# Pacing the gathers of sparse entries by the matmuls of two passes, and a finer ring of row buffers

## The chip, the cores and the metric

The kernel runs on one core of a Trainium2 chip. The time is the device time of one execution in microseconds (us), the median of several executions. A core has these engines: TensorE for matmuls (PE in the profile; PEld is its loading of weights), VectorE (DVE), ScalarE (ACT), GpSimd (POOL) and SyncE (SP), which in this kernel only issues transfers. Sixteen DMA engines move the data. Each engine works through its own instructions in order, and waits on semaphores for what others do.

## The reference, cut to what matters

The reference is a graph network of two layers on 3327 nodes with 512 features. The adjacency matrix `adj` (fp32, values in 0.05 to 1, about a quarter of a per cent of it nonzero, denser towards the first nodes) is given as a dense matrix; the kernel reads its transpose `adjT`.

```python
# layer 0
h = relu(layernorm(x))
u = h @ W1                                  # 512 -> 128
g = relu(adj @ u + b1)
x = x + (adj @ g) @ W2 + b2
# layer 1
h = relu(layernorm(x))
attn_a = sigmoid(concat([adj @ h, h], 1) @ Wa.T + ba)
attn_b = sigmoid(concat([adj @ h, h], 1) @ Wb.T + bb)
hw = h @ W_sa
scores = (hw @ a_sa[0, :512])[:, None] + (hw @ a_sa[0, 512:])[None, :]
e = where(adj != 0, exp(-leaky_relu(scores, 0.01)), 0)
x_a = (e / (e.sum(1, keepdims=True) + 1e-5)) @ hw
x_b = adj @ (h @ W_gcnb) + b_gcnb
return x + sigmoid(attn_a * x_a + attn_b * x_b)
```

Layer 0 needs two products with `adj`, and the second needs all of the first. Layer 1 needs, for each node, the rows `h` of its neighbours, weighted once by `adj` and once by an exponential of scores that is zero where `adj` is zero.

## The kernel before

The nodes are padded to 3328 = 26 blocks of 128. The columns of `adjT` are taken in seven chunks, six of 512 and a last one of 256.

**Pass 1 (lines 442 to 486)** computes `adj @ u`. For each chunk c it goes through the 26 blocks j: `load_adj` (L197, on the SP queue) brings a tile of 128 x 512 entries (256 KB) into one of eight buffers, TensorE adds `u[j]` times the tile to `acc_u` (L466), and VectorE reduces the same tile to `most` (L467): the largest magnitude in each group of 32 columns, so that it is known which rows have anything nonzero in which group. In chunk 0 the blocks of `x` are loaded, normalized and multiplied as well. After a chunk's last matmul, `make_g` (L252) makes gT from the sum on ScalarE (L256) and turns it with `pg` (L259).

**The lists.** `make_lists` (L335) is a generator that makes, out of `most` of one chunk, the lists of nonzero rows, while the tiles of the next chunk go by (one `next` per tile from j = 2 on; for chunk 6, during pass 2's chunk 0). The 128 nodes of a block i ≥ 1 are four groups of 32: the half of the partitions says which half of the block, and `q` (0 or 1) which of the two groups in that half. A block has a fixed number of *rounds*, `rooms[i]`: 10, 8, 7, 6, 6, then five blocks of 5, twelve of 4 and three of 3, together 119. One round of one q is 128 row numbers, one per partition: 64 rows for each of two groups. So there are 238 columns of numbers: `row_h` (which row of h) and `row_a` (which 32 entries of `adjT`, L428). As soon as a batch of lists is made, `make_lists` issues on GpSimd all of its gathers of entries (L432 to L439, recorded at L327): an indirect transfer each, of 128 pieces of 32 numbers (128 bytes), into `ae[i]`, which is kept for every block until layer 1. That makes 238 *gathers of entries*, queued by batches.

**Pass 2 (L553 to L576)** is the same walk over `adjT` with `g` in place of `u` (L558). When a chunk's sum is complete, `make_h1` turns it (px, L524), adds `x`, normalizes, and writes the rows of h (512 numbers and a score) to `h_dram` (L531).

**The hub.** Block 0 is the densest and is combined in full, with `adjT`'s first columns and all rows of h (`combine_hub`, L141, L577 to L590).

**Layer 1 (L634 to L756).** For block i ≥ 1, `combine(i)` goes through segments of at most four rounds. A segment takes one buffer `hr` of eight rows of 520 numbers per partition, of which there are three; GpSimd gathers two rows per partition and round (128 x 2080 bytes each, L327): 238 *row gathers*. Then VectorE adds the scores (L652, one operation per q), `masked_exp` (L130) makes the exponentials from them and from the entries in `ae[i]`, and four matmuls per round (L671), each on half of the partitions, add both weighted sums. `turn(i)` (L678) transposes the sums, `weigh(i)` (L712) multiplies by `W_sa` (`p_a`, L717) and `W_g` (`p_b`, L722), and `finish` (L601) makes the output. The three are pipelined: combine of block i, turn of block i−1, weigh of block i−2. `weigh` takes four banks of PSUM of the pool psB: p_s for the column sums of e, p_a, and two of p_b, whose second uses 257 of 512 columns at most.

The buffers of pools are recycled: an instruction that writes to a buffer waits for the last readers of what stood in it. Within an engine, the order is the order of the program text, except where a priority or `issue_after` says otherwise.

Of the kernel before, what the change touches and what calls it, by code (L numbers as in the profile page):

```python
# [43 lines left out]
def kernel(  # L44
# [71 lines left out]
    hubp = ctx.enter_context(tc.tile_pool(name="hubp", bufs=LAG + 2))  # L116

    def ln_relu(dst, src, pool, name):
        stats = pool.tile([P, 6], F32, tag="bn6", name=f"bn_{name}", bufs=3)
# [65 lines left out]
    with (  # L185
# [137 lines left out]
            for t in ae[1:]:  # L323
                nc.gpsimd.memset(t[:, :, :GW], 0.0)

        def gather(dst, table, rows, last):
            nc.gpsimd.indirect_dma_start(  # L327
                out=dst, out_offset=None, in_=table,
                in_offset=bass.IndirectOffsetOnAxis(ap=rows, axis=0),
                bounds_check=last, oob_is_err=False,  # L330
            )

        adj_groups = adjT.rearrange("j (b i) -> (j b) i", i=GW)

        def make_lists(c, most):  # L335


# [48 lines left out]
            for batch in batches:  # L386
                col = {}
                m = 0
                for i, q in batch:
                    col[i, q] = m  # L390
                    m += rooms[i]
                f0 = first[batch[0][0]] + batch[0][1] * rooms[batch[0][0]]
                pl = bank(psB, f"p_list_{f0}")
                plv = pl[:, : m * NT].rearrange("p (c j) -> p c j", j=NT)
                for i, q in batch:
                    r = rooms[i]
                    at = l0w.tile(
                        [P, max(rooms), 2, HALF], BF16, tag="at", name=f"at_{i}_{q}", bufs=3
                    )
# [25 lines left out]
                nc.vector.tensor_scalar(  # L425
                    row_h[:, f0 : f0 + m], jb[:, :m], float(NP - 1), None, op0=ALU.min
                )
                nc.vector.scalar_tensor_tensor(  # L428
                    row_a[:, f0 : f0 + m], jb[:, :m], float(NG), group_col[:, f0 : f0 + m],
                    op0=ALU.mult, op1=ALU.add,  # L430
                )
                for i, q in batch:  # L432
                    for k0, k1 in segments(i):
                        for k in range(k0, k1):
                            f = f0 + col[i, q] + k
                            gather(
                                ae[i][:, 2 * k0 + q * (k1 - k0) + k - k0, :GW], adj_groups,
                                row_a[:, f : f + 1], NP * NG - 1,
                            )  # L439
                yield  # L440

        for i in range(4):
# [8 lines left out]
        for c in range(NCH):  # L451
# [3 lines left out]
            for j in range(NB):  # L455
                if c == 0:
                    if j + 4 < NB:
                        load_x(j + 4)
                    if j + 3 < NB:
                        normalize(j + 3)  # L460
                    if j + 2 < NB:
                        turn_h(j + 2)
                    if j + 1 < NB:
                        make_u(j + 1)
                a = load_adj(j, c, "a1")
                nc.tensor.matmul(acc[:, :w], u[j], a[:, :w], start=(j == 0), stop=(j == NB - 1))  # L466
# [86 lines left out]
        for c in range(NCH):  # L553
            c0, w = chunks[c]
            acc = bank(psA, f"acc_g_{c}")
            for j in range(NB):
                a = load_adj(j, c, "a2")
                nc.tensor.matmul(  # L558
                    acc[:, :w], g[j], a[:, :w], start=(j == 0), stop=(j == NB - 1)
                )  # L560
# [66 lines left out]
    with tc.tile_pool(name="spw", bufs=2) as spw:  # L627
# [6 lines left out]
        def combine(i):  # L634
# [3 lines left out]
            r = rooms[i]  # L638
            acc = [bank(psA, f"acc_{i}_{h}") for h in range(2)]
            es = spw.tile([P, 2, GW], F32, tag="es", name=f"es_{i}")  # L640
            for k0, k1 in segments(i):
# [6 lines left out]
                both = ae[i][:, 2 * k0 : 2 * k1, :]  # L648
                e = both[:, :, GW:]
                s_l = s_left[i * P // CW][:, i % (CW // P), :].rearrange("p (q i) -> p q i", q=2)  # L650
# [16 lines left out]
                for k in range(n):  # L667
                    for q in range(2):
                        for h in range(2):
                            half_p = slice(h * HALF, (h + 1) * HALF)  # L670
                            nc.tensor.matmul(  # L671
                                acc[h][q * HALF : (q + 1) * HALF, :], both[half_p, q * n + k, :],
                                hr[half_p, q * n + k, :D],
                                start=(k0 + k == 0), stop=(k1 == r and k == n - 1),
                            )
            return acc, es

        def turn(i, ty, tyT):  # L678
# [16 lines left out]
                        tyT[:, :, h, :], pt.rearrange("p (k n) -> p k n", k=KD)  # L695
                    )

        def add_up(i, es):

            p_s = bank(psB, f"p_s_{i}")  # L700
            if i:
                for h in range(2):
                    half_p = slice(h * HALF, (h + 1) * HALF)
                    nc.tensor.matmul(
                        p_s[half_p, 0:1], es[half_p].rearrange("p q i -> p (q i)"), ones[half_p],
                        start=True, stop=True,
                    )
            else:
                nc.tensor.matmul(p_s[:, 0:1], es, ones, start=True, stop=True)
            return p_s  # L710

        def weigh(i, tyT, es):  # L712
            p_s = add_up(i, es)
            p_a = bank(psB, f"p_a_{i}")
            p_b = [bank(psB, f"p_b_{i}_{k}") for k in range(2)]
            for k in range(KD):
# [3 lines left out]
            for n in range(2):  # L720
                for k in range(KD):
# [1 line left out]
                        p_b[n][:, :WH], tyT[:, k, 0, :], W_g_sb[:, k, n * WH : (n + 1) * WH],  # L723
                        start=(k == 0), stop=(k == KD - 1),
                    )
            finish(spw, i, p_a, p_b, p_s[:, 0:1])

        turning, weighing = None, None
        for i in [*range(NB), None, None]:
# [15 lines left out]
                weigh(*weighing)  # L745
            weighing = (b, tyT, es) if turning is not None else None
            turning = made

    over = nc.values_load(overflow[0:1, 0:1], min_val=0, max_val=1)
    with tc.If(over > 0):  # L750
# [124 lines left out]
```

## Time and profile before

| | |
|---|---|
| median of 3 executions | 1151.23 us (1142.97 to 1166.88) |
| span of the profiled execution | 1129.3 us |
| busy: PE, DVE, POOL, PEld, ACT | 856.7, 530.2, 527.3, 422.6, 189.9 us |
| mean granted clock of TensorE | 0.868 |
| moved by DMA | 216.54 MB, 192 GB/s on average |

The stages, by the first and last instructions of their lines: chunk 0 of pass 1 to 88 us, chunks 1 to 6 to 447, a transition to pass 2's steady walk to 484, pass 2 to 667, the hub to 734, layer 1 to the end.

How to read the page: its slices are fortieths of the span (28.2 us), each digit the busy tenths of an engine, or the granted clock of TensorE in tenths (PEclk), or the share of time that the DMA engines are busy. In the groups, after the count come the busy time, the mean time of one instruction in ns, then the idle time of the engine right before these instructions and what ended most of it. "issue" means that the engine waited for nothing that the profile shows. "remote", or another core or an unknown queue, means that the releaser could not be named. A matmul in fp32 is recorded as two instructions, so 182 matmuls of a pass are 364.

### The profile page before, as it was taken

Reading aid. Unit: us, or ns where it says so; the run is one execution under the profiler, and the core shown is the slowest. Engines: PE = TensorE matmul, PEld = TensorE weight load, DVE = VectorE, ACT = ScalarE, POOL = GpSimd, SP = SyncE. Lnnn points to the kernel's source line nnn. Section 1 sums busy time; section 2 is a strip of 40 time slices with the busy share of each in tenths; the row PEclk is TensorE's granted clock in tenths of the full one; section 3 lists DMA queues with packets and bytes.
Section 4 is the critical chain, followed back from the end, with each engine's and each line's share of the span. In section 5 each row is a group of like instructions: output and inputs, shape, how many; then the busy total and the mean of one; then the engine's idle time right before and its main releaser. Section 6 shows DMA issues by size and latency. Waiting matters only on the chain.

```text
span 1129.3 us, 12108 instructions
## 1 busy us (share of the span) xinstructions
PE 856.7 (76%) x3639; PEld 422.6 (37%) x3639; DVE 530.2 (47%) x1593; ACT 189.9 (17%) x405; POOL 527.3 (47%) x559
## 2 busy tenths in 40 slices
PE   4898428256382917399999977858998989999996
PEld 3663103012030304144343443323554445555554
DVE  5656215234262715236566676412454444454543
ACT  4560000000000000002111131100222122223232
POOL 6543764736647464540000005166766676666400
PEclk9999657658586958599999999888999989999998
DMA  6797227144263514289999968676777777877511
GB/s 220 265 278 242 50 63 230 29 136 118 57 205 100 170 46 137 81 268 367 320 347 347 334 233 273 171 213 175 202 221 215 217 208 213 215 211 217 177 57 41
DMA packets 116105, 216.54 MB, mean 192 GB/s; under 512 B 18849, under 2 KB 32448, under 8 KB 116032
## 3 DMA queue, kind: packets, MB, share of 16 engines
q1 hardware_dynamic: 82368, 138.27, 37.8%
q0 software_dynamic: 26656, 66.41, 21.8%
q10 hardware_dynamic: 7008, 11.02, 2.8%
q8 instruction: 31, 0.51, 0.2%
q14 instruction: 42, 0.34, 0.1%
HBM read 189.14 MB, written 27.37 MB: 192 GB/s over the span
## 4 chain that ended last, share of the span: by engine, by line
another core or an unknown queue 22%; PE 22%; issue 16%; DMA 15%; POOL 14%; DVE 7%; ACT 2%; SPq 1%; POOLq 0%; ACTq 0%; DVEq 0%
POOL hr L327 12%; PE acc_g L558 9%; DMA a<-in_adjT_dram 8%; DMA hr<-h_rows,row_h 4%; PE acc_u L466 4%; PE p_a L717 2%; PE p_b L722 2%; PE acc L671 1%; DVE most L467 1%; PE px L524 1%; DMA xb<-x 1%; POOL x L230 1%; DMA x<-in_x_dram 1%; ACT hrow L128 1%
## 5 line engine op out<-in xcount | busy, mean ns | idle before, releaser
L327 POOL DMA_INDIRECT hr<-h_rows,row_h x238 | 243.6, 1024 | 324.3 <-DMA a_hub<-in_adjT_dram 184.6
L327 POOL DMA_INDIRECT ae<-in_adjT_dram,row_a x238 | 238.7, 1003 | 182.3 <-issue 70.1
L466 PE MATMUL acc_u<-a,u 128*128 128x512 f32 (+1 forms) x364 | 208.4, 694 | 91.7 <-DMA a<-in_adjT_dram 80.9
L467 DVE TENSOR_REDUCE most<-a 128x16 f32<-128x512 f32 (+1 forms) x182 | 112.6, 641 | 125.5 <-DMA a<-in_adjT_dram 123.8
L558 PE MATMUL acc_g<-a,g 128*128 128x512 f32 (+1 forms) x364 | 159.5, 590 | 9.5 <-DMA a<-in_adjT_dram 9.4
L671 PE MATMUL acc<-hr,ae 64*64 64x512 f32 x952 | 136.8, 624 | 26.5 <-issue 10.5
L466 PEld LDWEIGHTS acc_u<-a,u 128*128 128x128 f32 x364 | 71.3, 223 | 168.6 <-DMA a<-in_adjT_dram 115.4
L558 PEld LDWEIGHTS acc_g<-a,g 128*128 128x128 f32 x364 | 69.8, 198 | 88.4 <-issue 62.3
L717 PE MATMUL p_a<-W_sa_sb,tyT 128*128 128x512 f32 x208 | 97.1, 610 | 1.6 <-DVE f L608 1.2
L722 PE MATMUL p_b<-W_g_sb,tyT 128*128 128x257 f32 x416 | 94.7, 379 | 0.3 <-issue 0.3
L722 PEld LDWEIGHTS p_b<-W_g_sb,tyT 128*128 128x128 f32 x416 | 78.6, 189 | 23.2 <-issue 12.4
L652 DVE TENSOR_TENSOR ae<-s_left,hr 128x128 f32<-128x128 f32 (+2 forms) x72 | 19.4, 269 | 142.0 <-DMA hr<-h_rows,row_h 132.2
L671 PEld LDWEIGHTS acc<-hr,ae 64*64 64x64 f32 x952 | 44.6, 137 | 104.6 <-issue 82.7
L512 DVE SCALAR_TENSOR_TENSOR junk<-hrow,w_rows 128x512 f32<-128x512 f32 x104 | 71.5, 688 | 4.5 <-ACT hrow L128 1.9
L256 ACT ACTIVATE gT<-acc_u,b_col 128x512 f32<-128x512 f32 (+1 forms) x7 | 4.6, 657 | 374.8 <-remote 258.4
L259 PE MATMUL pg<-ident,gT 128*128 128x128 f32 x26 | 6.9, 410 | 78.8 <-ACT gT L256 61.8
L717 PEld LDWEIGHTS p_a<-W_sa_sb,tyT 128*128 128x128 f32 x208 | 37.7, 191 | 39.9 <-issue 38.2
L526 DVE TENSOR_TENSOR x<-px,xb 128x512 f32<-128x512 f32 x26 | 17.8, 684 | 67.8 <-PE px L524 58.9
L230 POOL TENSOR_TENSOR x<-x,b_row 128x512 f32<-128x512 f32 x26 | 32.9, 1276 | 34.9 <-ACT h L128 20.9
L415 DVE TENSOR_TENSOR past<-p_list,place_col 128x416 f32<-128x416 f32 (+7 forms) x17 | 9.1, 537 | 73.0 <-remote 51.2
L133 ACT ACTIVATE ae<-ae 128x256 f32<-128x256 f32 (+2 forms) x36 | 13.7, 379 | 155.4 <-DVE ae L132 79.1
L247 PE MATMUL pu<-W_sb,hT 128*128 128x128 f32 x208 | 31.1, 297 | 7.9 <-ACT hT L241 7.9
(126 smaller groups left out, 849.8 us busy)
## 6 DMA issues: line engine op xcount, KB each, us to landing
a<-in_adjT_dram SPq DMA_DIRECT2D x312, 256.0 KB
h_rows<-hrow SPq DMA_DIRECT2D x26, 260.0 KB
h_hub<-h_rows SPq DMA_DIRECT2D x26, 260.0 KB
x<-in_x_dram SPq DMA_DIRECT2D x26, 256.0 KB
xb<-x SPq DMA_DIRECT2D x26, 256.0 KB
xb<-xb SPq DMA_DIRECT2D x26, 256.0 KB
a<-in_adjT_dram SPq DMA_DIRECT2D x52, 128.0 KB
x<-x ACTq DMA_DIRECT2D x26, 256.0 KB
```

Source lines behind the costliest of these rows:

```text
L230: nc.gpsimd.tensor_tensor(xs[i], xs[i], b2_row, ALU.add)
L247: nc.tensor.matmul(pu[:, :HID], hT[:, k, :], W1_sb[:, k, :], start=(k == 0), stop=(k == KD - 1))
L327: nc.gpsimd.indirect_dma_start(out=dst, out_offset=None, in_=table, in_offset=bass.IndirectOffsetOnAxis(ap=rows, axis=0), bounds_check=las ...
L466: nc.tensor.matmul(acc[:, :w], u[j], a[:, :w], start=(j == 0), stop=(j == NB - 1))
L467: nc.vector.tensor_reduce(most[:, : w // GW, j], a[:, :w].rearrange("p (b i) -> p b i", i=GW), axis=AX.X, op=ALU.max, apply_absolute_value ...
L512: return nc.vector.scalar_tensor_tensor(junk, h, 1.0, w_rows[:, s, :], op0=ALU.mult, op1=ALU.mult, accum_out=into)
L526: nc.vector.tensor_tensor(x1, px, xi, ALU.add)
L558: nc.tensor.matmul(acc[:, :w], g[j], a[:, :w], start=(j == 0), stop=(j == NB - 1))
L652: nc.vector.tensor_tensor(e[:, q * n : (q + 1) * n, :], s_l[:, q, :].unsqueeze(1).to_broadcast([P, n, GW]), hr[:, q * n : (q + 1) * n, D : ...
L671: nc.tensor.matmul(acc[h][q * HALF : (q + 1) * HALF, :], both[half_p, q * n + k, :], hr[half_p, q * n + k, :D], start=(k0 + k == 0), stop= ...
L717: nc.tensor.matmul(p_a, tyT[:, k, 1, :], W_sa_sb[:, k, :], start=(k == 0), stop=(k == KD - 1))
L722: nc.tensor.matmul(p_b[n][:, :WH], tyT[:, k, 0, :], W_g_sb[:, k, n * WH : (n + 1) * WH], start=(k == 0), stop=(k == KD - 1),)
```

## The change

It has three parts.

1. **Gathers of entries are paced.** `make_lists` no longer issues them; it only notes which lists are ready (`listed`). A generator, `gather_adj`, yields them one at a time in the order in which layer 1 will need them. `gather_behind(matmul)` takes the next one and makes it wait for that matmul. Pass 1 calls it for every odd tile (one per two tiles; if the list in question isn't ready, the slot passes unused), pass 2 for three of each four tiles. What is left is issued in layer 1, two per block, behind the block's last row gather. What it is for: the gathers come one at a time among the tiles, rather than by batches in a row.
2. **Row buffers by rounds.** `hr` is now a buffer of two rows (one round), and there are 16 of them, 32 rows in place of 24. A buffer comes free when its round's four matmuls are done, rather than with the whole segment. The score addition is one operation per round, over both q.
3. **The column sum** p_s goes into the last column of the second p_b's bank, behind p_b's matmuls, so `weigh` takes three banks.

```diff
-        def gather(dst, table, rows, last):
...
+    listed = set()
+    def gather_adj():
+        for i in range(1, NB):
+            r = rooms[i]
+            for k0, k1 in segments(i):
+                for q in range(2):
+                    for k in range(k0, k1):
+                        while (i, q) not in listed:
+                            yield None
+                        f = first[i] + q * r + k
+                        yield gather(
+                            ae[i][:, 2 * k0 + q * (k1 - k0) + k - k0, :GW], adj_groups,
+                            row_a[:, f : f + 1], NP * NG - 1,
+                        )
+    columns = gather_adj()
+    def gather_behind(matmul):
+        g = next(columns, None)
+        if g is not None:
+            tc.add_manual_dep(
+                g.ins, matmul.ins.name,
+                mybir.DependencyInfo(mybir.DependencyClass.Sync, mybir.DependencyReason.DATA),
+                reason="pace",
+            )
...
-                for i, q in batch:
-                    for k0, k1 in segments(i):
-                        for k in range(k0, k1):
-                            f = f0 + col[i, q] + k
-                            gather(
-                                ae[i][:, 2 * k0 + q * (k1 - k0) + k - k0, :GW], adj_groups,
-                                row_a[:, f : f + 1], NP * NG - 1,
-                            )
+                listed.update(batch)
                 yield
...
                 if j >= 2:
                     next(lists, None)
+                if j % 2:
+                    gather_behind(added)
...
                 if c == 0 and j >= 2:
                     next(lists, None)
+                if (c * NB + j) % 4 != 3:
+                    gather_behind(added)
...
-                hr = spw.tile([P, 2 * SEG, ROW], F32, tag="hr", name=f"hr_{i}_{k0}", bufs=3)
+                hr = []
                 for k in range(n):
+                    hr.append(spw.tile([P, 2, ROW], F32, tag="hr", name=f"hr_{i}_{k0 + k}", bufs=16))
                     for q in range(2):
                         f = first[i] + q * r + k0 + k
-                        gather(hr[:, q * n + k, :], h_dram[:, :], row_h[:, f : f + 1], NP - 1)
...
-                for q in range(2):
+                        rows = gather(hr[k][:, q, :], h_dram[:, :], row_h[:, f : f + 1], NP - 1)
                     nc.vector.tensor_tensor(
-                        e[:, q * n : (q + 1) * n, :],
-                        s_l[:, q, :].unsqueeze(1).to_broadcast([P, n, GW]),
-                        hr[:, q * n : (q + 1) * n, D : D + 1].to_broadcast([P, n, GW]), ALU.add,
+                        e.rearrange("p (q k) i -> p k q i", q=2)[:, k],
+                        s_l, hr[k][:, :, D : D + 1].to_broadcast([P, 2, GW]), ALU.add,
                     )
...
-                                hr[half_p, q * n + k, :D],
+                                hr[k][half_p, q, :D],
...
+            with tc.issue_after(rows.ins):
+                for _ in range(2):
+                    next(columns, None)
...
-            p_s = add_up(i, es)
             p_a = bank(psB, f"p_a_{i}")
             p_b = [bank(psB, f"p_b_{i}_{k}") for k in range(2)]
...
-            finish(spw, i, p_a, p_b, p_s[:, 0:1])
+            p_s = p_b[1][:, CW - 1 : CW]
+            add_up(i, es, p_s)
+            finish(spw, i, p_a, p_b, p_s)
```

More of the change, by code (lines that the diff above doesn't have):

```diff
@@ L116, with gather @@
     hubp = ctx.enter_context(tc.tile_pool(name="hubp", bufs=LAG + 2))
+    def gather(dst, table, rows, last):
+        return nc.gpsimd.indirect_dma_start(
+            out=dst, out_offset=None, in_=table,
+            in_offset=bass.IndirectOffsetOnAxis(ap=rows, axis=0),
+            bounds_check=last, oob_is_err=False,
+        )
+    adj_groups = adjT.rearrange("j (b i) -> (j b) i", i=GW)
+    listed = set()
[20 more added lines that the diff above has]
+                reason="pace",
+            )
     def ln_relu(dst, src, pool, name):
@@ L324, in make_constants @@
                 nc.gpsimd.memset(t[:, :, :GW], 0.0)
-        def gather(dst, table, rows, last):
[L327 to L330, printed above, removed]
-            )
-        adj_groups = adjT.rearrange("j (b i) -> (j b) i", i=GW)
         def make_lists(c, most):
@@ L431, in make_lists @@
                 )
-                for i, q in batch:
-                    for k0, k1 in segments(i):
-                        for k in range(k0, k1):
-                            f = f0 + col[i, q] + k
-                            gather(
-                                ae[i][:, 2 * k0 + q * (k1 - k0) + k - k0, :GW], adj_groups,
-                                row_a[:, f : f + 1], NP * NG - 1,
-                            )
+                listed.update(batch)
                 yield
@@ L465 @@
                 a = load_adj(j, c, "a1")
-                nc.tensor.matmul(acc[:, :w], u[j], a[:, :w], start=(j == 0), stop=(j == NB - 1))
+                added = nc.tensor.matmul(
+                    acc[:, :w], u[j], a[:, :w], start=(j == 0), stop=(j == NB - 1)
+                )
                 nc.vector.tensor_reduce(
@@ L557 @@
                 a = load_adj(j, c, "a2")
-                nc.tensor.matmul(
+                added = nc.tensor.matmul(
                     acc[:, :w], g[j], a[:, :w], start=(j == 0), stop=(j == NB - 1)
@@ L640, in combine @@
             es = spw.tile([P, 2, GW], F32, tag="es", name=f"es_{i}")
+            s_l = s_left[i * P // CW][:, i % (CW // P), :].rearrange("p (q i) -> p q i", q=2)
             for k0, k1 in segments(i):
                 n = k1 - k0
-                hr = spw.tile([P, 2 * SEG, ROW], F32, tag="hr", name=f"hr_{i}_{k0}", bufs=3)
+                both = ae[i][:, 2 * k0 : 2 * k1, :]
+                e = both[:, :, GW:]
+                hr = []
                 for k in range(n):
+                    hr.append(spw.tile([P, 2, ROW], F32, tag="hr", name=f"hr_{i}_{k0 + k}", bufs=16))
                     for q in range(2):
                         f = first[i] + q * r + k0 + k
-                        gather(hr[:, q * n + k, :], h_dram[:, :], row_h[:, f : f + 1], NP - 1)
-                both = ae[i][:, 2 * k0 : 2 * k1, :]
-                e = both[:, :, GW:]
-                s_l = s_left[i * P // CW][:, i % (CW // P), :].rearrange("p (q i) -> p q i", q=2)
-                for q in range(2):
+                        rows = gather(hr[k][:, q, :], h_dram[:, :], row_h[:, f : f + 1], NP - 1)
                     nc.vector.tensor_tensor(
-                        e[:, q * n : (q + 1) * n, :],
-                        s_l[:, q, :].unsqueeze(1).to_broadcast([P, n, GW]),
-                        hr[:, q * n : (q + 1) * n, D : D + 1].to_broadcast([P, n, GW]), ALU.add,
+                        e.rearrange("p (q k) i -> p k q i", q=2)[:, k],
+                        s_l, hr[k][:, :, D : D + 1].to_broadcast([P, 2, GW]), ALU.add,
                     )
@@ L696, in turn, with add_up @@
                     )
-        def add_up(i, es):
-            p_s = bank(psB, f"p_s_{i}")
+        def add_up(i, es, p_s):
             if i:
@@ L704, in add_up @@
                     nc.tensor.matmul(
-                        p_s[half_p, 0:1], es[half_p].rearrange("p q i -> p (q i)"), ones[half_p],
+                        p_s[half_p, :], es[half_p].rearrange("p q i -> p (q i)"), ones[half_p],
                         start=True, stop=True,
@@ L708, in add_up @@
             else:
-                nc.tensor.matmul(p_s[:, 0:1], es, ones, start=True, stop=True)
-            return p_s
+                nc.tensor.matmul(p_s, es, ones, start=True, stop=True)
         def weigh(i, tyT, es):
-            p_s = add_up(i, es)
             p_a = bank(psB, f"p_a_{i}")
@@ L747 @@
             turning = made
+        assert next(columns, None) is None
     over = nc.values_load(overflow[0:1, 0:1], min_val=0, max_val=1)
```

## The prediction, made blind

> **What bounds the kernel now.** I read the page first: the slices, then the groups with their idle time, then the chain of waits.
>
> ```profile
> span 1129.3 us, 12108 instructions
> PE   4898428256382917399999977858998989999996
> POOL 6543764736647464540000005166766676666400
> DMA  6797227144263514289999968676777777877511
> L327 POOL DMA_INDIRECT ae<-in_adjT_dram,row_a x238 | 238.7, 1003 | 182.3 <-issue 70.1
> L256 ACT ACTIVATE gT<-acc_u,b_col 128x512 f32<-128x512 f32 (+1 forms) x7 | 4.6, 657 | 374.8 <-remote 258.4
> another core or an unknown queue 22%; PE 22%; issue 16%; DMA 15%; POOL 14%; DVE 7%; ACT 2%; SPq 1%; POOLq 0%; ACTq 0%; DVEq 0%
> ```
>
> Each slice is 28 us. Slices 4 to 16 are pass 1's chunks 1 to 6. There PE, DMA and GpSimd take turns: PE is low where POOL is high, and DMA is low with PE. No engine is the limit, and 22% of the chain is an unnamed releaser; it is what gT (each chunk's first step after its last matmul) waits for. The windows by stage (busy of PE, PEld, DVE, ACT, POOL with counts; granted clock; DMA share; GB/s):
>
> ```profile
> 88.00:447.00 359.00, 196.53 (x806) 79.85 (x804) 150.65 (x396) 4.09 (x6) 206.77 (x207) 0.70 0.42 119
> 447.00:484.00 37.00, 15.62 (x46) 6.43 (x44) 9.79 (x41) 0.47 (x1) 19.93 (x20) 0.68 0.38 104
> 484.00:667.00 183.00, 170.88 (x429) 77.82 (x429) 108.44 (x341) 30.70 (x67) 11.96 (x12) 0.98 0.96 329
> 734.00:949.00 215.00, 186.75 (x996) 91.74 (x996) 84.94 (x265) 42.54 (x87) 146.67 (x144) 0.93 0.72 208
> 949.00:1129.00 180.00, 167.93 (x892) 97.32 (x892) 85.15 (x254) 52.05 (x101) 76.52 (x74) 0.98 0.55 156
> ```
>
> So 359 us go to six chunks of the same matmuls that pass 2 does, seven of them, in 183. The timeline of PE and ACT in chunk 3 shows how:
>
> ```profile
> 286.19 2.08 PE L466 MATMUL acc_u<-a,u 128*128 128x512 f32 x2 [1.10 <-DMA a<-in_adjT_dram]
> 291.10 2.08 PE L466 MATMUL acc_u<-a,u 128*128 128x512 f32 x2 [2.83 <-DMA a<-in_adjT_dram]
> 296.58 2.07 PE L466 MATMUL acc_u<-a,u 128*128 128x512 f32 x2 [3.41 <-DMA a<-in_adjT_dram]
> 311.72 0.69 ACT L256 ACTIVATE gT<-acc_u,b_col 128x512 f32<-128x512 f32 x1 [67.45 <-remote]
> ```
>
> Tiles come one per 5 us. The chunk's last matmul ended at 298.7, yet gT began at 311.7. In between, POOL issues gathers of entries back to back (38 from 257.9 to 306.0, 1.00 us each and 0.30 between). There are seven such runs, and every late gT (168.9, 243.6, 311.7, 365.7, 423.8) comes a few us after one ends. The load of tile k waits for the matmul of tile k−8 to give its buffer back. I followed that lag tile by tile: nothing outside a run, rising from the run's fifth to ninth gather to as much as 40 us. So the news that a matmul has ended reaches the other queues late while gathers run; why, no view says.
>
> One stretch speaks for pacing. The run at 486.3 stands in pass 2:
>
> ```profile
> 484.40 15.72 PE L558 MATMUL acc_g<-a,g 128*128 128x512 f32 x36
> 486.00:501.00 15.00, 0.00 (x0) 0.00 (x0) 0.00 (x0) 0.00 (x0) 11.39 (x12) 1.00 0.91 291
> ```
>
> Eighteen tiles (36 halves) in 15.72 us, 0.87 each, beside twelve gathers (the second row counts entries' gathers alone), with no buffer late by more than 1.2 us. This is nearly the density the change gives pass 2, but short.
>
> **The Trainium skill.** "DMA: Bandwidth & Descriptors", Issuing engines are not separate DMA queues: DMAs of all issuers share the same 16 engines. The trace agrees that these matter in pass 2 (0.96) and not in the stalls, where their share falls to 0.13. "Perfetto Trace Analysis", DMA Instruction — SWDGE (GPSIMD): the profiled end of a GpSimd gather is the end of descriptor generation, not of the transfer. Fits: 1.00 us in the row, but 5 to 6 us to landing for row gathers in the chain. "TensorE: Matmul & The Clock Gate", The cost: per-tile semaphore tail: completion increments are drained one after another, about 26 ns each. After a run the trace shows a burst some 40 ns apart, but nothing in that section explains 13 us of delay.
>
> **The change, part by part.**
>
> *Pass 1.* No run is left: one gather per two tiles. POOL waits for the matmul of an odd tile; queued behind it are only further entries' gathers and then row gathers, needed much later. Undisturbed tiles are in chunk 3 before its run bites: tiles 1 to 15 start from 248.44 to 267.5, 1.36 us each (the lists' matmuls and DVE work lie between), and tiles 15 to 20 come every 0.88. A chunk is 15 × 1.3 + 11 × 0.88 = 29.2, say 29.5 us; chunk 6, half as wide, 26 × 0.7 = 18. Pass 1 ends at 88 + 5 × 29.5 + 18 = 254 instead of 447. It has 6 × 13 slots, less about four before the first lists (98.4), so 74 gathers.
>
> *Transition.* The 37 us to 484 hold a late gT (17 us) and another run of gathers. Ten tiles at 1.1 and the column products come to 13: 267.
>
> *Pass 2.* 182 × 3/4 = 137 gathers. Those at 90 to 470 show 17.9 us of 16-engine time for 226, 0.08 us each, so 11 us in a stage at 0.96 share. I charge half, 6 (0 to 15): 183 + 6 takes it to 456. POOL needs 1.30 of every 1.45 us, so it keeps up.
>
> *Hub.* The first row gather came 18.8 us after pass 2's end and the hub's end 48 us after that. Sixteen rounds of buffers now admit 32 gathers instead of 20 here; the 12 extra (266 KB each) contend with the hub's loads, +2. 456 + 19 + 48 + 2 = 525 instead of 734.
>
> *Layer 1.* Up to 949 it is bound by row gathers:
>
> ```profile
> 737.24 1.00 POOL L327 DMA_INDIRECT hr<-h_rows,row_h  x1 [24.83 <-PE acc L671]
> L327 POOL DMA_INDIRECT hr<-h_rows,row_h x238 | 243.6, 1024 | 324.3 <-DMA a_hub<-in_adjT_dram 184.6
> L717 PE MATMUL p_a<-W_sa_sb,tyT 128*128 128x512 f32 x208 | 97.1, 610 | 1.6 <-DVE f L608 1.2
> ```
>
> POOL stands 24.83 us with all buffers full until the hub is done. After that a gather comes every 1.32 us. From block 11 PE is the limit (167.93 busy of 180). To block 13 the layer needs 2 × (8+7+6+6+5×5+3×4) = 128 gathers after block 1's. Twelve are now ahead, 116 stay, and the 238 − 74 − 137 = 27 entries' gathers, two per block, come here: 143, less a few after block 13, 140 × 1.32 = 185, plus 8 for the last landing, scores and rounds, 193. So 215 becomes 193, then 180 as before. End: 525 + 193 + 180 = 898; 5 for a slower granted clock on a PE that now has no pauses gives 903. The page's span is 1129.3 and the median 1151.23, a factor 1.019: **about 918 us**.
>
> *Costed at nothing:* 119 score additions instead of 72, 47 × 0.22 (half-size rows of the 0.27 us group) = 10 us on a DVE that is busy 85 of 215 us there; the column sum moved into the last bank (PE idles 1.6 us in all before p_a, so the freed bank brings nothing and the later sum costs PE nothing, perhaps 0.1 us at the very end); the waits on POOL, released by 456, before the first row gather at 475. Their data is read only by the masked exponential in layer 1.
>
> **Rivals.**
>
> *B, gathers cost the passes the same wherever they stand.* The excess now is (447 − 254) + 24 = 217 us over 226 gathers, 0.96 each. If it is a price per gather, the 211 in the passes still cost 203; gain 14 there and 21 in layer 1: 1151 − 36 = 1115. For it: nobody has shown what delays the signals. Against: the first gathers of every run delay nothing, and the twelve in pass 2 cost 0.
>
> *C, pass 2 stalls (slower).* Three gathers per four tiles leave POOL 0.5 us in 4.4; over 183 us this may be a run like pass 1's, whose lag only rose from the fifth to ninth gather. If half of its tiles go at 5.5 instead of 1.1 us, 91 × 4.4 = 400 are added to 903: 1303, × 1.019 = 1328, of which some is spared, since the gathers wait for the late matmuls themselves: 1300. Against: the twelve at 486.3, and that self-limiting.
>
> *D, layer 1 loses.* The deeper buffers bring nothing since POOL, not buffers, is the limit, and the extra gathers come on top: 215 + 27 × 1.32 = 251 instead of 193, 903 + 58 = 961: about 975. For it: POOL is busy 147 of 215 us, and waits for buffers in layer 1 add to some 30 us beside the 24.83.
>
> **How the numbers follow.** A, as worked out, 0.70: 918. D 0.12, B 0.10, C 0.08. The range leaves out B, C and a little of A: its low end has 27 us chunks (−13), pass 2 free (−6), no clock loss (−5), a transition of 5 us (−8) and a factor of 1.0 (−17), 869; its high end is D (975) with pass 2 at +15 instead of +6 and the last 11 tiles of each chunk of pass 1 at 1.36 instead of 0.88 (+26): 1010. Faster by over 2%: A, D and 0.06 of B's 0.10, 0.88; within 2%: the rest of B (near 1128), 0.04; slower: C, 0.08.
>
> **What would show it.** Right: POOL's digits in pass 1 even, at 3 to 5; its idle time there ended by PE acc_u; gT within 1 or 2 us of the last matmul, and its 258.4 us for an unnamed releaser gone; PE's digits at 6 to 9 from slice 4 on; pass 1 ends near 254 and pass 2 near 456; the 24.83 us wait shrinks to about 9 (12 × 1.3 less). Wrong: gaps of 3 us before acc_u or acc_g while POOL is busy (B, C), pass 2 over 200 us, or block 13 ending over 215 us after the hub (D). The forecast is most exposed in one step: that the delay comes from gathers back to back and not from gathers as such.

## The result, and the profile after

The changed kernel takes **966.76 us** (963.49 to 969.22, median of 4) against 1147.19 beside it: ratio **0.844** (95% interval 0.838 to 0.849). Forecast: 918, with 869 to 1010 as range. A second set of runs of the same pair, made last, gave 965.11 against 1147.78, ratio 0.841 (0.834 to 0.848). The page of the changed kernel, with the slices, the two groups of gathers and the chain:

```profile
span 967.2 us, 12394 instructions
PE   4798999999889899887864946788998999999995
POOL 5651544456667766676375366766776766664000
DMA  6799898886889999997697566765666777776111
PE 51%; issue 15%; DMA 11%; DVE 10%; POOL 5%; another core or an unknown queue 3%; ACT 2%; SPq 1%; POOLq 0%; ACTq 0%; DVEq 0%
L119 POOL DMA_INDIRECT ae<-in_adjT_dram,row_a x238 | 250.7, 1053 | 167.2 <-PE acc_u L487 51.2
L119 POOL DMA_INDIRECT hr<-h_rows,row_h x238 | 242.2, 1018 | 146.9 <-PE acc L697 55.6
```

A slice is now 24 us. PE's digits are 8 and 9 through the passes (slices 3 to 18), and the unnamed releaser has gone from 22% of the chain to 3%. GpSimd's gathers of entries wait for acc_u, as the change asks. The groups of ScalarE show gT waiting for the matmul itself:

```profile
L293 ACT ACTIVATE gT<-acc_u,b_col 128x512 f32<-128x512 f32 (+1 forms) x7 | 4.6, 657 | 158.7 <-PE acc_u L487 158.7
```

In every chunk gT begins within 0.1 us or so of the chunk's last matmul; before, six of the seven came 2 to 24 us late. The windows by stage (PE, PEld, DVE, ACT, POOL busy with counts; clock; DMA share; GB/s): pass 1 from chunk 1, pass 2, the hub from the first row gather, layer 1 to block 13, the rest.

```profile
88.00:250.00 162.00, 153.20 (x808) 69.17 (x806) 149.48 (x400) 4.33 (x7) 77.66 (x76) 1.00 0.83 258
250.00:462.00 212.00, 187.87 (x473) 84.84 (x473) 118.13 (x379) 31.64 (x69) 144.29 (x135) 0.95 0.94 307
480.00:545.00 65.00, 42.30 (x82) 15.86 (x84) 26.13 (x109) 8.49 (x26) 34.02 (x34) 0.84 0.71 216
545.00:790.00 245.00, 201.89 (x997) 101.18 (x990) 86.01 (x289) 42.97 (x88) 166.77 (x164) 0.88 0.67 182
790.00:967.00 177.00, 164.81 (x891) 99.05 (x889) 85.21 (x263) 51.90 (x99) 65.54 (x64) 0.97 0.51 144
```

| until | before | forecast | measured |
|---|---|---|---|
| pass 1 ends | 447.4 | 254 | 249.7 |
| pass 2 ends | 667.4 | 456 | 461.6 |
| first row gather | 686.2 | 475 | 479.9 |
| hub ends | 734.2 | 525 | 544.6 |
| block 13 ends | 948.9 | 718 | 789.7 |
| end | 1129.3 | 898 + 5 | 967.2 |

The passes came as forecast. Nearly all of the 64 us by which the span was missed lies between the first row gather and block 13: the hub took 64.7 us, not 50 (48 before), and layer 1 to block 13 took 245, not 193 (215 before). There TensorE stands idle again, as it did in pass 1. The timeline of PE in the changed kernel shows the transposes of block 1, then those of the kernel before at the same place:

```profile
583.55 0.27 PE L712 MATMUL ptt<-ident,ty 128*128 128x128 f32 x1 [0.37 <-issue]
584.29 0.32 PE L712 MATMUL ptt<-ident,ty 128*128 128x128 f32 x1 [0.47 <-issue]
585.01 0.27 PE L712 MATMUL ptt<-ident,ty 128*128 128x128 f32 x1 [0.39 <-issue]
586.42 0.46 PE L712 MATMUL ptt<-ident,ty 128*128 128x128 f32 x1 [1.15 <-issue]
```
```profile
774.02 1.09 PE L683 MATMUL ptt<-ident,ty 128*128 128x128 f32 x8
```

Eight transposes in a row took 1.09 us; here single ones go out 0.7 to 2.1 us apart (the first four are shown), with nothing that the profile shows to wait for ("issue"). GpSimd had been gathering rows without a pause for most of the 38 us before.

### The profile page after: what moved, and what is told of

It is laid out like the page before. It is cut to its first block, busy times and chain, and to the rows that moved or that the text cites. A ratio compares the mean times of both kernels' runs of the same rounds, so it can differ in the third digit from the quotient of the medians.

```text
span 967.2 us, 12394 instructions
## 1 busy us (share of the span) xinstructions
PE 830.8 (86%) x3639; PEld 424.9 (44%) x3639; DVE 530.7 (55%) x1640; ACT 190.9 (20%) x405; POOL 537.9 (56%) x559
## 4 chain that ended last, share of the span: by engine, by line
PE 51%; issue 15%; DMA 11%; DVE 10%; POOL 5%; another core or an unknown queue 3%; ACT 2%; SPq 1%; POOLq 0%; ACTq 0%; DVEq 0%
PE acc_u L487 11%; PE acc L697 11%; PE p_b L748 8%; PE p_a L743 7%; PE acc_g L583 7%; DMA a<-in_adjT_dram 6%; POOL hr L119 4%; PE ptt L712 2%; DVE most L490 2%; DVE junk L537 2%; DMA hr<-h_rows,row_h 2%; DMA x<-in_x_dram 2%; PE px L549 2%; PE p_list L437 1%
## 5 line engine op out<-in xcount | busy, mean ns | idle before, releaser
L119 POOL DMA_INDIRECT ae<-in_adjT_dram,row_a x238 | 250.7, 1053 | 167.2 <-PE acc_u L487 51.2
L583 PE MATMUL acc_g<-a,g 128*128 128x512 f32 (+1 forms) x364 | 162.2, 598 | 18.7 <-DMA a<-in_adjT_dram 12.8
L697 PE MATMUL acc<-hr,ae 64*64 64x512 f32 x952 | 151.9, 650 | 28.4 <-issue 22.6
L487 PE MATMUL acc_u<-a,u 128*128 128x512 f32 (+1 forms) x364 | 167.1, 584 | 4.8 <-DMA a<-in_adjT_dram 2.4
L679 DVE TENSOR_TENSOR ae<-s_left,hr 128x64 f32<-128x64 f32 x119 | 25.8, 225 | 156.1 <-DMA hr<-h_rows,row_h 133.1
L697 PEld LDWEIGHTS acc<-hr,ae 64*64 64x64 f32 x952 | 57.7, 143 | 103.5 <-issue 96.4
L487 PEld LDWEIGHTS acc_u<-a,u 128*128 128x128 f32 x364 | 62.9, 191 | 52.4 <-issue 40.1
L196 PE MATMUL acc_hub<-h_hub,a_hub 128*128 128x512 f32 x52 | 31.2, 721 | 23.3 <-issue 21.3
L712 PE MATMUL ptt<-ident,ty 128*128 128x128 f32 x208 | 31.4, 288 | 9.5 <-issue 9.5
L651 DVE TENSOR_TENSOR va<-va,x1b 128x512 f32<-128x512 f32 x26 | 18.0, 692 | 37.7 <-ACT va L650 26.1
```

The source lines that it names most:

```text
L119: return nc.gpsimd.indirect_dma_start(out=dst, out_offset=None, in_=table, in_offset=bass.IndirectOffsetOnAxis(ap=rows, axis=0), bounds_ch ...
L196: nc.tensor.matmul(acc[k], s, hs[j][0][:, :D], start=(j == 0), stop=(j == NB - 1))
L487: added = nc.tensor.matmul(acc[:, :w], u[j], a[:, :w], start=(j == 0), stop=(j == NB - 1))
L583: added = nc.tensor.matmul(acc[:, :w], g[j], a[:, :w], start=(j == 0), stop=(j == NB - 1))
L697: nc.tensor.matmul(acc[h][q * HALF : (q + 1) * HALF, :], both[half_p, q * n + k, :], hr[k][half_p, q, :D], start=(k0 + k == 0), stop=(k1 = ...
L712: nc.tensor.transpose(pt[:, k * P : (k + 1) * P], ty[h][:, k * P : (k + 1) * P], ident)
```

## The experiments

**Is it the rate of the gathers, or the wait?** The first attempt put a small clearing on GpSimd behind each gather, but left its place in the queue open:

```diff
                             gather(
...
                             )
+                            nc.gpsimd.memset(idle, 0.0)      # 128 x 192
```

> The kernel before, with one edit: GpSimd clears a small buffer (128 x 192, about 0.29 us) behind each gather of entries, so that in a run they come every 1.6 us instead of 1.30. No gather waits for a matmul, and the rows' buffers are the old ones. Theory T (TensorE's signals and its own issue fall behind while gathers follow one another at 1.30 us, and don't at 1.6): pass 1 ends near 260 instead of 447, the gathers run on to about 480, layer 1 as before: about 925 to 950 us, ratio 0.81 to 0.83. Rival R (what helps is that a gather waits for a matmul, so that it can never run ahead; the rate alone is nothing): pass 1 still takes over 400, and the time is 1100 or more.

Measured: 1149.23 us, ratio 0.999 (0.996 to 1.002). It tells nothing of either theory: the profile shows the clearings gathered ahead of the gathers (19 in a row from 107.9 us), which still come every 1.30 us. So the order within an engine is not always that of the program text: the clearings, which depend on nothing else, were moved. The same slip spoilt its sister, the changed kernel with such a clearing behind each row gather:

> The changed kernel with the same clearing (about 0.29 us) behind each row gather, so that these come every 1.6 us. Theory T: TensorE no longer falls behind: hub about 50 us from the first row gather, up to block 13 about 223 (116 row gathers at 1.6 and 24 of entries at 1.3, plus 8) instead of 245: about 930 us, ratio to before 0.81. Rival D (the number of gathers sets layer 1, at so much each): 142 x 0.29 = 41 us more, about 1005.

Measured: 982.69, ratio 0.855 (0.849 to 0.860). 156 clearings, 40.5 us, stood in chunk 0, which ended at 100.2 us instead of 88.6; the row gathers kept their 1.30. Then both with the clearing pinned between one gather and the next:

```diff
...
-                            gather(
+                            tc.keep_in_program_order(gather(
...
-                            )
+                            ))
+                            tc.keep_in_program_order(nc.gpsimd.memset(idle, 0.0))
```

> The kernel before; behind each gather of entries GpSimd clears a small buffer (128 x 192, 0.26 us), now pinned in the queue between one gather and the next, so that in a run they come every 1.56 to 1.6 us instead of 1.30. No gather waits for a matmul. Theory T (it is the rate of 1.30 us that makes TensorE fall behind): pass 1 ends near 260 us instead of 447, gathers run on to about 480, 925 to 950 us, ratio 0.81 to 0.83. Rival R (the wait on the matmul does it; at 1.6 us without a wait TensorE falls behind as well): pass 1 takes over 400, time 1100 us or more.

Measured: **972.59, ratio 0.851 (0.844 to 0.858)**. No gather waits for a matmul here; the timeline of POOL shows the difference, a gather every 1.44 us:

```profile
99.55 1.00 POOL L328 DMA_INDIRECT ae<-in_adjT_dram,row_a  x1 [0.17 <-issue]
100.55 0.27 POOL L441 MEMSET idle<- 128x192 f32 x1
100.98 1.00 POOL L328 DMA_INDIRECT ae<-in_adjT_dram,row_a  x1 [0.17 <-issue]
```

So with 0.14 us more between gathers, and no wait, the kernel as a whole gains nearly what the change gains. Rival R, that only the wait helps, is out. But pass 1 itself is not put right. Single executions ran from 963 to 1001 us, and the profiled one took 1001; its pass 1 ends at 328.5:

```profile
87.00:329.00 242.00, 182.16 (x807) 79.98 (x806) 152.15 (x400) 4.12 (x6) 203.21 (x317) 0.84 0.61 176
```

That is 242 us, against 359 before and 162 in the changed kernel, at a clock of 0.84. If the whole excess of that execution lies in pass 1, pass 1 ends near 300 in the median one (an estimate: 328.5 less 1001.3 − 972.6), so theory T's 260 is missed too. The total is good because the rest is shorter than in the changed kernel: the hub takes 50.4 us and layer 1 to block 13 takes 214.2, with the old row buffers and no gathers of entries left. The lag of a load behind the later of the matmul and the reduction that free its buffer was up to 37 us before (chunks 2 to 6); it is up to 8 here and under 1 in the changed kernel. Whether it is the longer interval that helps, or the clearing itself between two gathers, was not separated.

**Is a wait enough without a lower rate?** A gather behind each tile of pass 1:

```diff
-                if j % 2:
-                    gather_behind(added)
+                gather_behind(added)
...
-                if (c * NB + j) % 4 != 3:
+                if j % 2 == 0:
```

> The changed kernel with a gather of entries behind every tile of pass 1 and every second tile of pass 2, none left in layer 1. In pass 1 a tile takes 1.1 us, less than a gather's 1.30, so GpSimd is never idle, though each gather still has to wait for its matmul. Theory T (rate): TensorE falls behind and pass 1 ends at 290 or later; the wait only lets it catch up now and then. Rival R (a wait on a matmul is enough): pass 1 ends near 250 as in the changed kernel, and the time is 935 or less.

Measured: 992.95, ratio 0.874 (0.867 to 0.881). The window of its pass 1:

```profile
87.00:319.00 232.00, 180.29 (x808) 80.48 (x808) 150.77 (x400) 4.12 (x6) 151.00 (x150) 0.85 0.63 183
```

232 us, not 162, though every gather waits for a matmul; its clock is down to 0.85. It isn't 359 either: the lag behind the matmul alone stays under 9 us in chunks 1 to 5, though it reaches 18 in chunk 6. That the late matmuls hold up the next gathers fits this, but was not tried apart. The mean interval of the gathers in pass 1 orders the paced kernels: 1.48 us here and 232 us, 1.56 in the run below with two gathers per three tiles and 173, 1.99 in the changed kernel and 162.

**What does the deep ring do, alone and taken away?** The old row buffers in the changed kernel, then the new ones in the kernel before:

```diff
...
-                    hr.append(spw.tile([P, 2, ROW], F32, tag="hr", name=f"hr_{i}_{k0 + k}", bufs=16))
+                hr = spw.tile([P, 2 * SEG, ROW], F32, tag="hr", name=f"hr_{i}_{k0}", bufs=3)
...
```

> The changed kernel with the old row buffers (three of eight rows, a score addition per q): pacing alone. Theory T (the deep ring lets GpSimd gather without a pause, and TensorE falls behind in the hub and in layer 1's first blocks): the hub takes about 48 us from the first row gather instead of 65, layer 1 up to block 13 about 235 to 250, the time 940 to 955 us. Rival D (layer 1 is longer because of 27 more gathers alone, and the deep ring brings the 21 us that were forecast): about 985.

Measured: **957.27, ratio 0.834 (0.829 to 0.840)**, some 9 us less than with the ring, though the two intervals just overlap. The hub takes 50.7 us from the first row gather (475.8 to 526.5), layer 1 to block 13 takes 247.4.

> The kernel before with the new row buffers alone (16 of one round, a score addition per round). The passes stay as they were. Theory T: hub some 15 us longer, layer 1 not shorter, 1150 to 1170 us, ratio 1.00 to 1.02. The prediction's own step (12 gathers ahead save 16 us, the ring costs nothing): about 1130, ratio 0.98.

Measured: 1164.9, ratio **1.014 (1.008 to 1.020)**. The hub takes 61.2 us instead of 48.0, layer 1 to block 13 takes 217.5 instead of 214.7. The ring costs 13 us in the hub and gives nothing clear after it.

**Is it the run of row gathers that delays the hub?** The changed kernel with the row gathers spaced by the pinned clearing:

> The changed kernel; behind each row gather GpSimd clears the same small buffer, pinned, so that row gathers come every 1.56 to 1.6 us. Theory T (rate): TensorE no longer falls behind: the hub ends about 52 us after the first row gather instead of 65, block 13 about 223 after it (116 row gathers at 1.59, 24 of entries at 1.30, plus 8) instead of 245, time 930 us. Rival D (so much per gather): 116 x 0.29 = 34 us more, about 1000.

Measured: 954.58, ratio 0.841 (0.834 to 0.848; the kernel before took 1134.83 on this chip), as a ratio no better than the changed kernel. The windows from the first row gather to the hub's end, in the changed kernel 65 us at PE 42 busy:

```profile
475.00:528.00 53.00, 39.09 (x84) 14.85 (x86) 27.36 (x110) 8.68 (x27) 43.14 (x66) 0.94 0.90 272
528.00:771.00 243.00, 198.19 (x994) 100.60 (x986) 87.26 (x290) 42.50 (x88) 205.16 (x305) 0.90 0.69 183
```

The hub is right: 52.2 us from the first row gather, as expected, with as many gathers ahead and with DMA's share at 0.90, more than the changed kernel's 0.71. Layer 1 is not: 243.5 to block 13, not 223. In the waits of that stretch, the first line is the changed kernel's, the second this one's:

```profile
PE ptt L712 <- issue: 9.5, 11, 1.7
```
```profile
PE ptt L715 <- issue: 2.4, 6, 0.5
```

The transposes hardly crawl any more, yet the stage is as long. GpSimd's waits for row buffers, in the same two kernels, show why:

```profile
POOL hr L119 <- PE acc L697: 38.6, 9, 21.8
POOL hr L120 <- PE acc L700: 8.2, 7, 2.9
```

The last number of each line is one wait that began in the hub. Without it, some 17 us of waits have shrunk to 5, and those for an unnamed releaser from 16 to 1. But each of the stage's 142 row gathers now comes 0.14 us later, 20 us in all. So the spacing costs about what it gives back.

**Is it the number of gathers?** Two gathers per three tiles in pass 1, so that none is left for layer 1:

```diff
-                if j % 2:
+                if j % 3 != 2:
```

> The changed kernel with two gathers of entries per three tiles in pass 1 instead of one per two: all 238 fit into the two passes, none is left in layer 1. Layer 1 to block 13 then has 27 gathers fewer: 27 x 1.3 = 35 us. If POOL is the limit there, 245 becomes 210 and the time is 932 to 940; if TensorE falling behind is the whole of it, 245 stays above 235 and the time is 955 to 967. Pass 1: at a gather per 1.6 to 1.7 us it should stay below 265.

Measured: **939.33, ratio 0.828 (0.822 to 0.835)**, the best that was measured where the kernel before takes 1135 or more. Its windows of the hub and of layer 1 to block 13:

```profile
484.00:549.00 65.00, 45.84 (x85) 17.07 (x87) 26.19 (x111) 8.69 (x27) 32.20 (x32) 0.76 0.73 222
549.00:759.00 210.00, 185.08 (x994) 97.39 (x986) 84.20 (x287) 42.37 (x87) 144.17 (x142) 0.90 0.75 209
```

210.8 us, 34 fewer than the changed kernel's 245.1, for 22 gathers fewer in the stretch (142 against 164), or 27 fewer in all: at 1.30 us each, 29 to 35. Pass 1 pays 12 us for taking them in (261.4), the hub keeps its 64.

**Order of ScalarE's queue.** In the changed kernel, exponentials of up to three segments of later blocks stand ahead of the copy of a block's sums; block 2's sums, complete at 583.2, were copied at 600.9, behind an exponential of block 4 at 597.5. An edit put the copies first. A second run joined this to two gathers per three tiles in pass 1 and to pinned clearings behind the row gathers of blocks 1 and 2. A third had the old ring with none left:

```diff
...
-                masked_exp(e, both[:, :, :GW])
+                done = copies.get(i - 1 if k0 else i - 2)
+                with tc.issue_after(done.ins) if done is not None else nullcontext():
+                    masked_exp(e, both[:, :, :GW])
...
+                copies[i] = copied
```

> The changed kernel with ScalarE's queue reordered in layer 1: the exponentials of a block's first segment are queued behind the copy of the sums (ty) of two blocks earlier, those of its second segment behind the copy of the block before. In the changed kernel up to three segments of later blocks stand ahead of a copy, so that the copy, and the banks that it frees, wait for rows of later blocks. Theory O (this order is what took the deep ring's gain): copies start within some 5 us of a block's last matmul instead of 5 to 18, block 13 ends about 225 after the hub instead of 245, time about 947. Theory T alone (TensorE falls behind at back-to-back gathers whatever ScalarE does): 958 to 967.

> The changed kernel with three edits at once: two gathers of entries per three tiles in pass 1 (none left in layer 1), the row gathers of blocks 1 and 2 alone spaced by the pinned clearing of a small buffer, and ScalarE's copies ahead of the exponentials of later blocks. Theory T gives 12 us in the hub beside the 27 of none left; theory O another 10 or so: about 915. If both are one and the same gain: about 927.

> The pacing with the old row buffers and two gathers of entries per three tiles in pass 1, none left in layer 1. From the run with pacing alone (hub 51 us from the first row gather, block 13 at 247 after it) less 27 gathers x 1.3 = 35 us in layer 1, plus 12 us in pass 1: about 935. With the effective price of the changed kernel's pair (deep ring, with and without the 27: 28 us less overall) it would be about 928.

Measured: 915.88, 882.62 and 894.6. But the kernel before took **895.5** beside them (888.83 to 898.55, 15 runs) on this chip, while the four other sets of runs had 1135 to 1152. The ratios are 1.027 (1.020 to 1.033), 0.986 (0.980 to 0.992) and 1.000 (0.997 to 1.003). Only ratios within this chip can be used, and none of the expectations in us is tested. The third says most: pacing, with old buffers and none left in layer 1, shows no gain here. Its passes end at 245.7 and 446.4. Since the whole is the same, the kernel before can hardly have stalled in pass 1 on this chip; its trace there was not taken.

But the trace of the first of the three has the deep ring and its row gathers, at the same 1.30 us. The windows are its hub, its layer 1 to block 13, and the same stage of the third; then what TensorE waited for in the hub, in the changed kernel (480 to 545) and here (462 to 512):

```profile
462.00:512.00 50.00, 37.23 (x82) 14.32 (x84) 23.70 (x101) 7.10 (x23) 33.83 (x34) 0.97 0.87 285
512.00:732.00 220.00, 175.59 (x994) 89.59 (x986) 85.23 (x293) 41.21 (x89) 166.25 (x164) 0.89 0.73 201
512.00:710.00 198.00, 168.49 (x995) 88.57 (x994) 82.37 (x263) 42.39 (x87) 148.14 (x144) 0.94 0.79 224
```
```profile
PE acc_hub L196 <- issue: 21.3, 5, 9.6
PE acc_hub L197 <- DMA h_hub<-h_rows: 12.8, 8, 2.6
```

The hub takes 50 us, not 65, with 34 gathers in a row as in the changed kernel, and the waits for nothing named ("issue") are gone. So gathers at 1.30 us without a pause are not enough to hold TensorE up: something that differs between chips or sessions belongs to it.

The copies did come first: those of blocks 1 and 2 within 0.1 us of the last matmul, 15 and 18 in the changed kernel. But there is also a slip: block 1's later segments were queued behind the hub's copy, and block 1 took 18 us instead of about 10. So what the order is worth stays open. The first run is 2.7% slower than the kernel before, and the combination gains 1.4%, where there is no stall to remove.

The last run was the changed kernel again, on one more chip:

> The changed kernel itself once more, unchanged, because the kernel before took 1135 to 1152 us beside the first eight runs but 895 us on the chip of the last three, where it can't have stalled. If this chip is like that one: the passes end where the run with none left has them (446), no stall is left to remove, the 27 gathers in layer 1 and the deep ring cost their 13 to 28 us, and the changed kernel is slower than before, ratio 1.01 to 1.04. If this chip is like the first ones: ratio 0.84 to 0.85 as in the result.

Measured: 965.11 against 1147.78, ratio 0.841 (0.834 to 0.848), as in the result. Pass 1 ends at 249.3, the hub takes 66.0 us, layer 1 to block 13 takes 244.9. How the changed kernel, without a further edit, does on the chip without stalls was not measured.

## Why the prediction was right, point by point

*Pass 1 and the transition: right in size, and in mechanism as far as tested.* 249.7 for 254, and pass 2's first matmul at 250.7. The step that it called most exposed, "the delay comes from gathers back to back and not from gathers as such", is what the pinned spacing and the run with a gather per tile show, on the chips that stall. The end of a run is not what ends the delay, though: of the late gT that the prediction puts a few us behind a run's end, the one at 365.7 comes 0.2 us before it, and the last, at 465.0, some 8 us before. Rival B is out: paced, 211 gathers in the passes cost little.

*Pass 2 with its transition: 10 us too little.* 212 us from pass 1's end to its own, with 135 gathers, where 202 were forecast. On the chip without stalls it took 199 to 202. The lag reaches 7.5 us in the last chunk, so C's fear was real in kind. It stays there; but in the run with a gather per tile it was not held under 9 everywhere, so "self-limiting" is only partly borne out.

*Hub: the term "+2" should have been +17.* It was priced as bytes that contend for DMA. But DMA's share is 0.71 here, and in the two runs where the hub takes 50 to 52 us with as many gathers ahead it is 0.87 and 0.90. What costs is the unbroken run of 34 gathers at 1.30 us on a chip that stalls, the very thing that the first step had found in pass 1 and that this step didn't ask about. Old ring 50.7, spaced rows 52.2, deep ring 61 to 66. For the same reason a sign failed: the wait of 24.83 us at the hub's end was to shrink to about 9, and took 21.8; on the chip without stalls it took 7.2.

*Layer 1 to block 13: the step that failed.* 193 forecast, 245 measured, and with it the sign that was named for D, "block 13 ending over 215 us after the hub". The sum took gathers still to come, times 1.32, plus 8. Two of its terms are wrong:

- *The count.* It let the twelve gathers ahead at the start be saved. But a deeper ring is also fuller at the end: the stage saw 144 row gathers before and 142 after, and with 22 of entries 164, where 140 were counted. At 1.30 us the other 24 are 31 us.
- *The waits.* 164 × 1.30 is 213, so 32 of the 245 us are not gathers but, nearly all, waits between them, most of them for row buffers; before, it was 28 of 215. On the chip without stalls the same remainder is 7 us (220 with 164 gathers) and 11 (198 with 144): there "plus 8" is about right, with the gathers counted as they were issued.

Put the kernel before into that sum: 128 × 1.32 + 8 = 177, against 215 in the window. It was 38 us short on the very row that it was taken from, and part of this was booked as a gain. Rival D's way, 215 plus the 27 gathers at 1.32, gives 251, and is right within 6; without the 27 the stage takes 211, with the old ring and them 247.

*The end, and luck.* 177.5 for 180. The factor from span to median, 1.019, was not repeated (966.8 for a span of 967.2). This has nothing to do with the change, and took back some 15 us of the 64. Also, the result lies nearer to D's 975, which had a chance of 0.12, than to the 918 of the main line; the range holds it because its high end was built on D. Of the sums, 903 × 1.019 is 920 and D's 961 × 1.019 is 979; neither slip matters.

*Costed at nothing.* The score additions take 6.4 us more (25.8 instead of 19.4), not 10, and DVE's total is unchanged (530.7 for 530.2). The moved column sum has left PE's idle time before p_a under 1 us; it was not tried alone.

*The Trainium skill.* That a gather's profiled end is only the end of its descriptors ("Perfetto Trace Analysis", DMA Instruction — SWDGE (GPSIMD)) agrees with the run with the copies first: its row gathers landed 3.6 to 5.6 us after their start (those whose landing the trace has), against 1.00 us in the row. The figure of about 26 ns per completion ("TensorE: Matmul & The Clock Gate", The cost: per-tile semaphore tail) is too small: the wait of 11.79 us shown below would take some 450 of them in a row (an estimate from that page's figure), and only 14 matmuls are recorded during it.

*Open.* Why TensorE and those that wait for it are held up at 1.30 us between gathers, and less at 1.44; why one chip shows no loss, or whether it was a condition of that session; and the order on ScalarE. The granted clock falls in the stalls, but did not start the one in chunk 3 before: VectorE already waits, from 267.5 us on, for list matmuls that ended then, while the clock stays at 1.00 until 275:

```profile
279.29 0.38 DVE L415 TENSOR_TENSOR past<-p_list,place_col 128x208 f32<-128x208 f32 x1 [11.79 <-remote]
252.00:275.00 23.00, 19.27 (x114) 8.04 (x113) 11.67 (x33) 0.00 (x0) 13.13 (x14) 1.00 0.54 153
275.00:316.00 41.00, 15.39 (x21) 4.57 (x21) 13.56 (x29) 0.69 (x1) 24.73 (x25) 0.50 0.29 77
```

## What to carry to other kernels

Look for work that nobody waits for, but that runs beside the work that counts: in a trace where an engine's completions reach others late, find which other queue is busy in just those stretches, and first thin it out a little before building waits into it. Check a price formula on the row it comes from, by putting the kernel before into it, before using it on the kernel after. And what is found in one stage (here, unbroken runs of gathers) has to be asked of each other stage that a change lengthens or deepens. Count work that runs ahead at both ends of a stage: a deeper ring starts ahead and ends ahead. And measure before and after side by side on more than one chip, since the whole gain can be absent on one.

## What the runs showed of the hardware

On the chips where the kernel before took 1135 to 1152 us (four sets of runs), gathers of 128 rows on GpSimd, one per 1.30 us without a pause, went with buffers coming free up to 37 us after their last reader and with slow issue on TensorE (0.7 to 2.1 us between independent transposes). DMA's share was 0.13 to 0.37 in 28 us slices of pass 1's stalls. A 0.27 us clearing between two gathers made the interval 1.44 us; the lag then stayed within 8 us, though pass 1 still took 242 us in the profiled execution, not 162. On one chip, where the kernel before took 895 us, pacing made no difference that could be measured, and a run of 34 gathers at 1.30 us left TensorE no such wait.
